# Row maxima by a transposing transfer of three BF16 parts, exponentials four slots behind, FFN weights summed one part per slot

## The chip, the cores and the metric

The kernel runs on one core of a Trainium2 chip. A core has five engines that follow their own instruction streams and wait for each other by semaphores: TensorE (PE, with its weight loads shown as PEld), VectorE (DVE), ScalarE (ACT), GpSimd (POOL) and SyncE (SP, which here only issues transfers). Transfers are carried out by 16 DMA engines. The metric is the device time of one execution in microseconds (us); lower is better. A run's time is a little longer than the span of the instructions that the profiler records.

## The reference, cut to what matters

One transformer layer in FP32 on x of 2 x 1024 tokens x 512: attention with 32 heads of 16, then an FFN with quantised activations and ternary weights.

```python
q, k, v = (proj(w_q), proj(w_k), proj(w_v))          # from layernorm(x), 32 heads of 16
scores = jnp.einsum('bhqd,bhkd->bhqk', q, k) / jnp.sqrt(jnp.float32(D_K))
attn = jax.nn.softmax(scores, axis=-1)
out = jnp.einsum('bhqk,bhkd->bhqd', attn, v)
x = x + jnp.einsum('bse,oe->bso', out.transpose(0, 2, 1, 3).reshape(B, S, HIDDEN), w_o)
xq = int4_quant(layernorm(x))                        # per token
w_q = jnp.clip(jnp.round(w / (mean(abs(w)) + EPS)), -1.0, 1.0)   # for each of the three FFN weights
gate = jnp.square(jax.nn.relu(bitlinear(xq, w_gate, s_gate)))
inter = int8_quant(bitlinear(xq, w_up, s_up) * gate)
x = x + bitlinear(inter, w_down, s_down)
```

What matters for this case: softmax subtracts, in exact arithmetic, any number per query; the kernel subtracts the row's maximum, which it must know before the first exponential of that row. The FFN weights need mean(abs(w)) over the whole matrix before they can be made ternary.

## The kernel before, in words

The attention is cut into 32 steps (batch, half of the queries, group of 8 heads, and one of two head sets of 4). A step has 512 queries, 1024 keys and 4 heads, one head per strip of 32 rows of the PE array. Each step is cut into 8 slots. The main loop runs over slots T, and in each slot it writes out, for every engine, the work of three steps at different stages:

- **Maxima** of step n in slots 8n to 8n+7 (`max_mm` L590, `max_reduce` L600): per slot two PSUM tiles `psm` of 128 queries x 2 heads x 512 keys. PE writes them with queries on the partitions (two passes, for a high and a low part of q), and DVE reduces each to negated maxima, collected in `pm`.
- **Maxima into rows** (`max_parts` L602-608, `max_rows` L610-617). The exponentials have keys on the partitions and queries along the free axis, so the maxima, which stand one query per partition, must be turned into rows. In slot 8n+8 DVE combines the two key halves into `m` and writes two FP32R parts (the rounded value and what is left) into columns 32r and 32r+1 of `mcols`. At the end of slot 8n+9 PE turns the four 128-column blocks by matmuls with an identity (`psn`, L613), in one of the three rotating PSUM tiles that `pse` and `psm` use, and ACT copies the result to `mrow` (L617).
- **Exponentials** of step n from slot 8n+LE, with LE = 8 + LEAD and LEAD = 2 (`exp_mm` L630, `exponentials` L634): two PSUM tiles `pse` per slot, each of 128 keys x 2 heads x 512 queries, in three passes l: k times the high and the low part of q, and as the last pass a row of ones times the two rows of `mrow`, which subtracts the maximum. ACT takes exp of a whole tile into `e`.
- **Values** one slot later (`weigh_values` L660): `pso` accumulates e times v, with a column of ones for the denominators. After the last slot of a step ACT copies it to `po`; `normalise` (L672-699) sends the denominators through memory and multiplies on POOL.

A slot is written in this order (main loop, L1400-1445): the loads that are due, `max_parts` where it is due, one mixed group of scores (`pse` of one half beside `psm` of the other, on disjoint row strips, passes interleaved), `pso` of the slot before, a short piece of other work, the second mixed group, `max_rows` where it is due, and then `fill.run`. In slots before LE there are only maxima, in the last LE slots only exponentials.

**Other work** is handed out by `Fillers`: projections (`psq`, `psk` L476, `psv` L533), the output projection (`psy` L847), the FFN (`pg`, `pu` L937, `py` L1006), each a generator that yields estimated PE time or a gap, counted in calls of `run`, of which a mixed slot makes two. `pace` spreads the PE time over the slots that are left, at least 960 and at most 1800 ns a slot. The due times contain LEAD.

**Loads.** `load_k` (L567) and `load_q` (L573) of step n are written at slot 8n-5 into `kst` (3 buffers) and `qst` (6, two per step), so they overwrite step n-3; all tiles wait by themselves for the last reader of the buffer. `load_v` (L578) is written at slot 8n+5 (8n+8 for n under 8). All of these, the transposing transfers `xqT` (L919) and `iqT` (L1000), the projections' weights (L457) and `normalise`'s transfers stand in one SP queue, in the order in which they are written; SP issues them one after the other, and a transfer that waits holds up those behind it. The DMA rings also take SP's transfers in order.

**FFN weights.** `weight_sums` (L757-776) loads 35 parts of 256 KB or less by POOL, ACT sums each one's absolute value, four loads ahead, with ("gap", 1) between parts; then follow `weight_means` and `weight_quant`.

`the_end` (L1043) is the last FFN, after all slots, by a planner of its own.

Of the kernel before, what the change touches and what calls it, by code (L numbers as in the profile page):

```python
# [10 lines left out]
F32 = mybir.dt.float32  # L11
F32R = mybir.dt.float32r
BF16 = mybir.dt.bfloat16
# [3 lines left out]
ALU = mybir.AluOpType  # L17
# [4 lines left out]
P = 128  # L22
# [211 lines left out]
def kernel(  # L234
# [28 lines left out]
    nc = tc.nc  # L263
# [6 lines left out]
    QB = 512  # L270
    NQ = S // QB
    TQ = QB // P
    FC = (I + P - 1) // P
    SCALE = 0.25
    LEAD = 2

    WARM = 24

    const = ctx.enter_context(tc.tile_pool(name="const", bufs=1))
    sb = ctx.enter_context(tc.tile_pool(name="sb", bufs=1))  # L280
    sp = ctx.enter_context(tc.tile_pool(name="sp", bufs=3))
# [13 lines left out]
    identr = const.tile([P, P], F32R, name="identr")  # L295
    nc.vector.tensor_copy(identr, eye)
    ident = identr.bitcast(F32)
    onesr = const.tile([P, P], F32R, name="onesr")
    nc.vector.memset(eye, 1.0)
    nc.vector.tensor_copy(onesr, eye)  # L300
# [10 lines left out]
    negmagic = const.tile([P, 1], F32, name="negmagic")  # L311
    nc.vector.memset(negmagic, -MAGIC)

    mcols = [const.tile([P, TQ, P], F32R, name=f"mcols{k}") for k in range(2)]
    vst = [const.tile([P, 2, 4, 4, 32], F32, name=f"vst{k}") for k in range(1)]
    for m in mcols:
        nc.gpsimd.memset(m.bitcast(F32), 0.0)
    for v in vst:
        for s in range(2):
            nc.gpsimd.memset(v[:, s, :, :, 16 * (1 - s) : 16 * (1 - s) + 16], 1.0)  # L320
# [15 lines left out]
    def scores_psum(name):  # L336
        return ps_s.tile([P, 2, QB], F32, tag="s", name=name)
# [222 lines left out]
    pm, mrow, probs = {}, {}, {}  # L560
# [41 lines left out]
    def max_parts(n):  # L602
        m = sp.tile([P, TQ, 4], F32, tag="m", name=f"m_{n}")
        p = pm.pop(n)
        nc.vector.tensor_tensor(m, p[:, :, 0, :], p[:, :, 1, :], ALU.min)
        cols = mcols[n % 2].rearrange("p t (r c) -> p t r c", r=4)
        nc.vector.tensor_copy(cols[:, :, :, 0], m)
        nc.vector.tensor_tensor(cols[:, :, :, 1], m, cols[:, :, :, 0].bitcast(F32), ALU.subtract)

    def max_rows(n):  # L610
        ps = scores_psum(f"psn_{n}")[:, 0, :]
        for t in range(TQ):
            nc.tensor.matmul(  # L613
                ps[:, t * P : (t + 1) * P], mcols[n % 2][:, t, :], identr, start=True, stop=True
            )
        mrow[n] = sb.tile([P, QB], F32R, tag="mrow", name=f"mrow_{n}", bufs=2)
        nc.scalar.copy(mrow[n], ps)  # L617

    probs = {}

    def exp_mm(n, i, j, ps, l):
        for r in (2 * j, 2 * j + 1):
            rows = slice(32 * r, 32 * r + 32)
            if l < 2:
                left, right = kst[n][rows, i * P : (i + 1) * P], qst[n][l][rows, :]
            else:

                rows = slice(32 * r, 32 * r + 2)
                left, right = onesr[rows, :], mrow[n][rows, :]
            nc.tensor.matmul(ps[:, r % 2, :], left, right, start=(l == 0), stop=(l == 2))  # L630

    def exponentials(n, i, j, ps):
# [117 lines left out]
    def load_raw(m, i, name):  # L750
        ap, parts = mats[m]
        c, n, rows, cols = parts[i]
        t = sb.tile([P, 512], F32, tag="raw", name=f"{name}{m}_{c}_{n}", bufs=4)
        nc.gpsimd.dma_start(t[:rows, :cols], ap[c * P : c * P + rows, n : n + cols])
        return t

    def weight_sums():  # L757
        for m in range(3):
            wsum[m] = const.tile([P, 12], F32, name=f"wsum{m}")
            nc.gpsimd.memset(wsum[m], 0.0)  # L760
        todo = [(m, i) for m in range(3) for i in range(len(mats[m][1]))]
        raw = deque()
        for k in range(len(todo) + 4):
            if k >= 4:
                m, i = todo[k - 4]
                c, n, rows, cols = mats[m][1][i]
                junk = sb.tile([P, 512], BF16, tag="junk", name=f"junk{m}_{i}", bufs=1)
                nc.scalar.activation(
                    junk[:rows, :cols],
                    raw.popleft()[:rows, :cols],  # L770
                    AF.Abs,
                    accum_out=wsum[m][:rows, i : i + 1],
                )
            if k < len(todo):
                raw.append(load_raw(*todo[k], "raw"))
            yield ("gap", 1)

    def weight_means():
        tot = sp.tile([P, 3], F32, tag="wtot", name="wtot")
# [499 lines left out]
    for k, ap in enumerate((s_gate, s_up, s_down)):  # L1279
        t = const.tile([P, 1], F32, name=f"scale{k}")  # L1280
# [5 lines left out]
    ps = scores_psum("warm")  # L1286
    for k in range(WARM):
        nc.tensor.matmul(
            ps[:, k % 2, :], onesr, mcols[0].rearrange("p t c -> p (t c)"), start=True, stop=True
        )  # L1290
    fill.kind = "s"
    now(firsts[0])
# [40 lines left out]
    for b in range(B):  # L1333
# [12 lines left out]
        for g in range(NG):  # L1346
            n = first_step[b, 0, g]
# [8 lines left out]

    LE = NT + LEAD
    NSTEP = len(steps)
# [8 lines left out]
    for b in range(B):  # L1367
        for h in range(NQ):
            last = b == B - 1 and h == NQ - 1

            by = min(NT * (first_step[b, h, 0] + 4 * NG) + 40, NT * NSTEP + LEAD)
            ready = [f"norm_{b}_{h}_{g}" for g in range(NG - last)] + ["wo"]
# [3 lines left out]
            for tiles in ((0, 1), (2, 3)) if b == B - 1 else (tuple(range(TQ)),):  # L1376
                name = f"out_{b}_{h}_{tiles[0]}"
# [21 lines left out]
    left = 0.0  # L1399
    for T in range(LE + NT * NSTEP + 1):  # L1400
        fill.slot = T
        ne, ie = divmod(T - LE, NT)
        nm, im = divmod(T, NT)
        nw, iw = divmod(T - LE - 1, NT)

        fill.scores = int(T < LE - 1 or T >= NT * NSTEP)

        n = T // NT + 1
        if 1 < n < NSTEP and T == load_slot(n):
            b, h, g, s = steps[n]  # L1410
            fill.ensure(f"k_{b}_{g}_0", f"k_{b}_{g}_1", f"q_{b}_{g}_{h}")
            places(n)
            load_k(n)
            load_q(n)
        n = (T - 5) // NT
        if 0 <= n < NSTEP and T == due_v(n):
            b, h, g, s = steps[n]
            fill.ensure(f"v_{b}_{g}_0", f"v_{b}_{g}_1")
            load_v(n)
        if im == 0 and 0 < nm <= NSTEP:  # L1420
            max_parts(nm - 1)
        exps = [(ne, ie, j) for j in range(2)] if 0 <= ne < NSTEP else []
        maxs = [(nm, im, j) for j in (1, 0)] if nm < NSTEP else []
        mixed = bool(exps and maxs)
        if mixed:
            scores(exps[:1], maxs[:1])
        elif exps:
            scores(exps, [])
        if 0 <= nw < NSTEP:
            weigh_values(nw, iw)  # L1430
            if iw == NT - 1 and nw % 2 and nw < NSTEP - 1:
                b, h, g, _ = steps[nw]
                fill.add(f"norm_{b}_{h}_{g}", normalise(nw), (), "back")
            if iw == NT - 1 and nw == NSTEP - 2:
                fill.add("tokens", first_tokens(nw), (), "ffn", 0)
        feed()
        fill.run(100.0, short=True)
        if mixed:
            scores(exps[1:], maxs[1:])
        elif maxs:  # L1440
            scores([], maxs)
        if im == 1 and 0 < nm <= NSTEP:
            max_rows(nm - 1)
        share = min(max(fill.pace([w[4:] for w in ffns]), SHARE), MORE)
        left = fill.run(share + min(left, SHARE))

# [51 lines left out]
```

## Time and profile before

| | |
|---|---|
| median of 3 runs | 1182.28 us (1181.44 to 1182.52) |
| the profiled execution | 1181.5 us, span 1179.7 us, mean granted TensorE clock 0.999 |
| PE busy | 1154.8 us (98%) |
| DVE busy | 868.8 us (74%) |
| ACT busy | 686.8 us (58%) |
| POOL busy | 264.1 us (22%) |
| SP's transfers | 105.75 MB, 34.6% of the 16 DMA engines' span |
| `psn` matmuls, L613 | 128, busy 21.2 us, mean 288 ns |
| `mrow` copies on ACT, L617 | 32, busy 18.6 us, mean 582 ns |
| `pse<-mrow` matmuls, L630 | 1024, busy 203.9 us, mean 396 ns |

How to read it: busy time of PE is the union of modelled intervals; matmuls overlap, so a mean of 396 ns is a latency and not a price. The price of a matmul is read from the step from one start to the next. "Idle before" tells how long an engine stood before an instruction and what ended that; it costs nothing on an engine that is not the bottleneck.

### The profile page before, as it was taken

The page shows a single profiled execution, that of the slowest core. Times are in us where ns is not written, and L with a number is a line of the kernel's source. Part 1 is how long each engine was busy: PE and PEld are TensorE (multiplying, and loading weights), DVE is VectorE, ACT ScalarE, POOL GpSimd, SP SyncE. Part 2 cuts the span into 40 slices and gives each one's busy share as a digit, 9 for nine tenths or more (in the row PEclk, how much of TensorE's full clock was granted, in tenths as well). Part 3 has the DMA queues.
Part 4 walks back from the last instruction along what each step waited for, and adds up shares of the span by engine and source line. Part 5 has one row for each costly group of instructions (what it writes and reads, how often), then busy time and mean ns, then how long its engine had stood idle before and what let it go on. Part 6 is the DMA issues. An engine that isn't in the chain of part 4 may idle for free.

```text
span 1179.7 us, 21990 instructions
## 1 busy us (share of the span) xinstructions
PE 1154.8 (98%) x8922; PEld 522.5 (44%) x8922; DVE 868.8 (74%) x1261; ACT 686.8 (58%) x878; POOL 264.1 (22%) x319
## 2 busy tenths in 40 slices
PE   8899999999999999999999999999999999999998
PEld 5454444544444444544444445444444433444344
DVE  6765577898876677788866665786988788888467
ACT  2058765556565556566665555465666555665746
POOL 3224336465501101221011011022110001220111
PEclk9999999999999999999999999999999999999999
DMA  5666765556623323443633324244442516362300
GB/s 157 174 183 194 249 197 176 172 190 197 194 93 96 103 55 110 113 95 77 94 86 121 124 59 147 84 130 138 84 97 60 89 53 83 58 81 55 79 9 37
DMA packets 97099, 135.35 MB, mean 115 GB/s; under 512 B 34829, under 2 KB 54285, under 8 KB 96997
## 3 DMA queue, kind: packets, MB, share of 16 engines
q1 hardware_dynamic: 87204, 105.75, 34.6%
q0 software_dynamic: 9792, 28.19, 7.7%
q8 instruction: 70, 1.15, 0.4%
q14 instruction: 33, 0.26, 0.1%
HBM read 89.25 MB, written 37.19 MB: 107 GB/s over the span
## 4 chain that ended last, share of the span: by engine, by line
PE 81%; DVE 5%; DMA 5%; issue 2%; POOL 2%; SPq 2%; ACT 2%; POOLq 0%; DVEq 0%; ACTq 0%
PE pse L630 25%; PE pso L660 18%; PE psm L590 9%; PE psv L533 4%; PE psk L476 4%; PE psy L847 4%; PE psq L476 4%; PE pu L937 2%; PE py L1006 2%; DVE pm L600 2%; PE pg L937 2%; DMA rden<-rD 1%; PE psn L613 1%; SPq L505 1%; PE end L1161 1%
## 5 line engine op out<-in xcount | busy, mean ns | idle before, releaser
L600 DVE TENSOR_REDUCE pm<-psm 128x2 f32<-128x1024 f32 x512 | 623.8, 1222 | 242.9 <-PE pse L630 146.0
L634 ACT ACTIVATE e<-pse 128x1024 f32<-128x1024 f32 x512 | 522.7, 1023 | 408.2 <-PE pse L630 307.3
L590 PE MATMUL psm<-kst,qst 32*128 32x512 f32 x2048 | 369.5, 444 | 7.3 <-DMA kst<-kD 3.8
L630 PE MATMUL pse<-qst,kst 32*128 32x512 f32 x2048 | 367.6, 442 | 3.9 <-DVE pm L600 3.1
L630 PEld LDWEIGHTS pse<-qst,kst 32*128 32x128 f32 x2048 | 149.2, 183 | 332.8 <-issue 199.7
L660 PE MATMUL pso<-e,v 128*32 128x512 f32 x2048 | 272.9, 605 | 0.0
L630 PE MATMUL pse<-mrow,onesr 2*128 2x512 f32 x1024 | 203.9, 396 | 0.0
L590 PEld LDWEIGHTS psm<-kst,qst 32*128 32x128 f32 x2048 | 151.3, 183 | 25.5 <-ACT e L634 10.8
L630 PEld LDWEIGHTS pse<-mrow,onesr 2*128 2x128 f32 x1024 | 94.5, 183 | 3.3
L951 POOL TENSOR_TENSOR g<-g 128x460 f32<-128x460 f32 (+1 forms) x36 | 34.7, 964 | 244.7 <-ACT g L947 237.4
L660 PEld LDWEIGHTS pso<-e,v 128*32 128x32 f32 x2048 | 40.4, 108 | 94.4 <-issue 93.7
L807 POOL TENSOR_SCALAR low<-raws,whalf 128x512 bf16<-128x512 f32 (+2 forms) x35 | 52.0, 1488 | 30.5 <-DMA raws<-in_wuT 8.1
L476 PE MATMUL psq<-xnT,wq 128*128 128x512 f32 x112 | 57.8, 626 | 0.0
L533 PE MATMUL psv<-wv,xnT 128*128 128x128 f32 x384 | 53.2, 285 | 0.0
L533 PEld LDWEIGHTS psv<-wv,xnT 128*128 128x128 f32 x384 | 45.9, 191 | 12.5 <-issue 11.7
L847 PE MATMUL psy<-wo,OT 128*128 128x512 f32 x96 | 49.6, 625 | 0.0
L476 PE MATMUL psk<-xnT,wk 128*128 128x512 f32 x96 | 49.5, 624 | 0.0
L699 POOL TENSOR_TENSOR OT<-po,rden 128x512 f32<-128x512 f32 x15 | 19.2, 1278 | 99.5 <-PE pse L630 52.8
L547 POOL DMA_DIRECT2D vD<-vst x30 | 16.7, 559 | 110.5 <-ACT vst L545 107.8
L909 POOL TENSOR_SCALAR xn<-x,mv,a 128x512 f32<-128x512 f32 x12 | 25.1, 2089 | 71.5 <-DVE a L885 71.5
L937 PEld LDWEIGHTS <-xqT 128*128 128x128 bf16 x288 | 22.4, 98 | 37.8 <-issue 23.8
L937 PE MATMUL pg<-wg,xqT 128*128 128x460 fp8e4 (+1 forms) x144 | 34.2, 360 | 0.0
(227 smaller groups left out, 945.1 us busy)
## 6 DMA issues: line engine op xcount, KB each, us to landing
v<-vD SPq DMA_DIRECT2D x32, 512.0 KB
kst<-kD SPq DMA_DIRECT2D x31, 512.0 KB
qst<-qD SPq DMA_DIRECT2D x60, 256.0 KB
vD<-vst POOLq DMA_DIRECT2D x30, 256.0 KB, 5.7
qD<-hi_q SPq DMA_DIRECT2D x28, 256.0 KB
qD<-lo_q SPq DMA_DIRECT2D x28, 256.0 KB
x<-in_x SPq DMA_DIRECT2D x20, 256.0 KB
rden<-rD SPq DMA_DIRECT2D x15, 256.0 KB
```

What stands on the lines that cost most here:

```text
L476: nc.tensor.matmul(ps, w[:, c, :], xnT[b, h][:, c, :], start=(c == 0), stop=(c == KC - 1))
L533: nc.tensor.matmul(ps[:, i * P : (i + 1) * P], xnT[b, half][:, c, i * P : (i + 1) * P], w[:, c, :], start=(c == 0), stop=(c == KC - 1),)
L590: nc.tensor.matmul(ps[:, r % 2, :], qst[n][l][rows, t * P : (t + 1) * P], kst[n][rows, kh * QB : (kh + 1) * QB], start=(l == 0), stop=(l = ...
L600: nc.vector.tensor_reduce(pm[n][:, t, kh, 2 * j : 2 * j + 2], ps, AX.X, ALU.max, negate=True)
L630: nc.tensor.matmul(ps[:, r % 2, :], left, right, start=(l == 0), stop=(l == 2))
L634: nc.scalar.activation(e, ps, AF.Exp, scale=SCALE)
L660: nc.tensor.matmul(acc[n][32 * r : 32 * r + 32, :], vt[n][:, i, r, :], e[r // 2][:, r % 2, :], start=(i == 0), stop=(i == NT - 1),)
L807: nc.gpsimd.tensor_scalar(low, w, h[:rows, m, 1:2], None, ALU.is_lt)
L847: nc.tensor.matmul(ps, OT[b, h, g][:, i * P : (i + 1) * P], wo[g], start=(g == 0), stop=(g == NG - 1),)
L909: nc.gpsimd.tensor_scalar(xn, xt, mean, a, ALU.subtract, ALU.mult)
L937: nc.tensor.matmul(ps, xT[:, c, :], w[:, c, n : n + size], start=(c == 0), stop=(c == KC - 1))
L951: nc.gpsimd.tensor_tensor(g2[j], g2[j], g2[j], ALU.mult)
```

## The change

LEAD goes from 2 to 4, so every exponential stands four slots behind the last maxima of its step instead of two, and the due times that contain LEAD move with it. The maxima are written as three BF16 parts instead of two FP32R ones: `max_parts` now has five instructions (combine, BF16 copy, rest, BF16 copy of the rest, second rest) where it had three, and ends with a transposing transfer of `mcols` (128 x 512 BF16) to `mrow` on SP. `max_rows`, with its four matmuls, its PSUM tile and ACT's copy, is gone. The last pass of the exponentials has BF16 operands: three rows of `mrow` and three rows of BF16 ones. `weight_sums` has ("gap", 2) between parts, which in mixed slots is one part per slot instead of two. The warm-up matmuls use the BF16 tiles.

```diff
-    LEAD = 2
+    LEAD = 4
@@
+    onesb = const.tile([P, P], BF16, name="onesb")
+    nc.vector.memset(onesb, 1.0)
@@
-    mcols = [const.tile([P, TQ, P], F32R, name=f"mcols{k}") for k in range(2)]
+    mcols = [const.tile([P, TQ * P], BF16, name=f"mcols{k}") for k in range(2)]
@@ def max_parts(n):
-        cols = mcols[n % 2].rearrange("p t (r c) -> p t r c", r=4)
+        cols = mcols[n % 2].rearrange("p (t r c) -> p t r c", t=TQ, r=4)
+        rest = sp.tile([P, TQ, 4], F32, tag="rest", name=f"rest_{n}", bufs=1)
         nc.vector.tensor_copy(cols[:, :, :, 0], m)
-        nc.vector.tensor_tensor(cols[:, :, :, 1], m, cols[:, :, :, 0].bitcast(F32), ALU.subtract)
-
-    def max_rows(n):
-        ps = scores_psum(f"psn_{n}")[:, 0, :]
-        for t in range(TQ):
-            nc.tensor.matmul(
-                ps[:, t * P : (t + 1) * P], mcols[n % 2][:, t, :], identr, start=True, stop=True
-            )
-        mrow[n] = sb.tile([P, QB], F32R, tag="mrow", name=f"mrow_{n}", bufs=2)
-        nc.scalar.copy(mrow[n], ps)
+        nc.vector.tensor_tensor(rest, m, cols[:, :, :, 0], ALU.subtract)
+        nc.vector.tensor_copy(cols[:, :, :, 1], rest)
+        nc.vector.tensor_tensor(cols[:, :, :, 2], rest, cols[:, :, :, 1], ALU.subtract)
+        mrow[n] = sb.tile([P, TQ, P], BF16, tag="mrow", name=f"mrow_{n}", bufs=2)
+        nc.sync.dma_start_transpose(mrow[n], mcols[n % 2])
@@ def exp_mm(n, i, j, ps, l):
-                rows = slice(32 * r, 32 * r + 2)
-                left, right = onesr[rows, :], mrow[n][rows, :]
+                rows = slice(32 * r, 32 * r + 3)
+                left, right = onesb[rows, :], mrow[n][rows].rearrange("p t q -> p (t q)")
@@ def weight_sums():
-            yield ("gap", 1)
+            yield ("gap", 2)
@@ the warm-up
-            ps[:, k % 2, :], onesr, mcols[0].rearrange("p t c -> p (t c)"), start=True, stop=True
+            ps[:, k % 2, :], onesb, mcols[0], start=True, stop=True
@@ the main loop
-        if im == 1 and 0 < nm <= NSTEP:
-            max_rows(nm - 1)
```

## The prediction

> **What bounds the kernel now.** First the page's busy times, then the waits of PE, then the chain of work that ended last, then PE's timeline over three neighbouring slots, then SP's timeline.
>
> ```profile
> PE 1154.8 (98%) x8922; PEld 522.5 (44%) x8922; DVE 868.8 (74%) x1261; ACT 686.8 (58%) x878; POOL 264.1 (22%) x319
> ...
> PE 81%; DVE 5%; DMA 5%; issue 2%; POOL 2%; SPq 2%; ACT 2%; POOLq 0%; DVEq 0%; ACTq 0%
> ```
> ```profile
> PE psm L590 <- DMA kst<-kD: 3.8, 1, 3.8
> PE warm L1288 <- DVE lowrow L304: 3.6, 1, 3.6
> PE psm L590 <- ACT e L634: 3.2, 5, 0.9
> ```
>
> PE waits for others some 20 us in all, and the longest of it is one late `kst`. So the kernel is a row of PE instructions, and a slot costs what PE does in it. The timeline of slots 96 to 98 shows this to a hundredth (starts in us; each slot opens with a `pse<-qst,kst`):
>
> ```profile
> 423.57 0.50 PE L630 MATMUL pse<-qst,kst 32*128 32x512 f32 x2
> ...
> 428.28 0.50 PE L630 MATMUL pse<-qst,kst 32*128 32x512 f32 x2
> ...
> 430.17 0.50 PE L630 MATMUL pse<-qst,kst 32*128 32x512 f32 x2
> ...
> 431.09 0.66 PE L613 MATMUL psn<-identr,mcols 128*128 128x128 f32 x4
> 431.59 1.07 PE L847 MATMUL psy<-wo,OT 128*128 128x512 f32 x2
> 432.60 0.50 PE L630 MATMUL pse<-qst,kst 32*128 32x512 f32 x2
> ...
> 434.50 0.50 PE L630 MATMUL pse<-qst,kst 32*128 32x512 f32 x2
> 434.74 0.50 PE L590 MATMUL psm<-kst,qst 32*128 32x512 f32 x2
> 434.83 0.41 PE L630 MATMUL pse<-qst,kst 32*128 32x512 f32 x2
> 435.06 0.40 PE L630 MATMUL pse<-mrow,onesr 2*128 2x512 f32 x1
> ...
> 435.40 1.13 PE L847 MATMUL psy<-wo,OT 128*128 128x512 f32 x2
> 436.46 0.49 PE L630 MATMUL pse<-qst,kst 32*128 32x512 f32 x2
> ```
>
> Slot 96 (two `psy` matmuls) takes 4.71 us, slot 97 (`psn` and one `psy`) 4.32, slot 98 (one `psy`) 3.86. A mixed group (434.50 to 435.40) takes 0.90 us: three passes of `pse` in a chain, steps of 0.33 and 0.23, then 0.34 to the next shape. All 246 mixed slots fall on such prices: without other work 2.95, and 0.86 for each further matmul of 512 FP32 columns.
>
> **Part 1: `psn` goes.** Slot 97 against 98 prices it at 0.46; over the run, like slots with and without it differ by 0.45 (4.30 against 3.86, 4.34 against 3.90). Thirty lie in mixed slots, 13.5 us; one among maxima alone and one among exponentials alone, 0.35 each. **-14.2 us**. The 21.2 us of L613's busy time is not the price, because its latency overlaps the next matmuls. ACT loses 32 copies of 582 ns, 18.6 us, off the path: ACT is 58% busy.
>
> **Part 2: two more DVE instructions a step.** Three become five; the new ones are like L607 (207 ns) and L608 (230 ns), so 32 x 0.44 = 14 us on DVE. They stand ahead of slot 8n+8's reductions. DVE's reduction (1222 ns, two a slot, 2.44 of some 3.9 us) idles 243 us before it; the reductions cover the cost only while this lasts. Between 0 and +14; taken 0, since those waits are PE's.
>
> **Part 3: the way to `mrow`.** After the last reduction (1.2 us) five small DVE instructions (1.0), the transfer's issue on SP (the like-sized `xqT`, L919, 1.21 at the median, 7.55 once), landing 4.5 us after the issue at the median by the trace's semaphore events, 14.2 at worst. That is some 8 us, and four slots give 15.5. Taken 0; a transfer as slow as the worst would hold the third pass some 2 us, and with it PE. The wait has another side: SP now stands at each slot 8n+8 until DVE is done. Before, SP ran ahead: step 1's `v` was issued at 73.5 us, 13.7 us before its slot began. What stands behind it are weights (L457) used at least two slots later, and stores; priced in part 5. The 32 issues are 39 us of SP's time, which mostly waits.
>
> **Part 4: LEAD 4.** Mixed slots fall from 246 to 244; maxima alone and exponentials alone gain two slots each. The two mixed slots (10 and 11) cost 3.85 and 3.88. As slots of maxima alone they are DVE's: two reductions and a little, 2.6 (36 to 40 us: 2.66 to 2.79 with twice the other work), 5.2. Two slots of exponentials alone with nothing beside cost 1.90 and 2.15 near 1105 us; taken 3.8. 5.2 + 3.8 - 7.7 = **+1.3**. No reason excludes a gain: with other work in them these late slots cost 1.65 plus that work, so between +0.8 and +1.8.
>
> **Part 5: the loads of `kst` and `qst`.** With LEAD 4 the last exponentials of step n-3 stand in slot 8n-5, the same slot at whose head step n's load is written, where before they stood in 8n-7. So the load can start two slots later than before. SP's timeline for step 14, whose load waited for exactly that event before:
>
> ```profile
> 464.05 0.57 SPq L567 DMA_DIRECT2D kst<-kD  x1
> 464.66 1.11 SPq L573 DMA_DIRECT2D qst<-qD  x2
> 465.87 3.57 SPq L680 DMA_DIRECT2D dD<-po  x2
> ```
>
> The last `qst` lands at 478.9, 14.8 us after 464.05 (last semaphore event of that transfer). Step 14's maxima begin at 490.3, and the exponentials of slot 107 (8n-5) end at 472.6: from there, where the load now starts, 17.6 us remain. For steps 10 to 31 the loads take 13.9 to 19.9, median 14.8, and the window measured in this way is 16.4 to 21.6, median 17.6: mostly hidden with 2 to 3 us to spare. For steps 3 to 9 the loads take 17.0 to 24.8, because FFN weights travel beside them or their `qD` stores land late, and windows are 16.7 to 18.9. I take 3 us of stall at step 4 (its `q` store lands at 139.5, with 1 MB of x ahead in the rings), 1 each at 6 and 8, and 4 at step 9: the changed program's order puts batch 1's first `wv` behind step 9's loads and uses it in slot 70, some 12.5 us after those can start, while a transfer behind them lands when they do, 16 to 17 later. **+9**, between 0 (every load as in steps 10 to 31) and +35 (rival A). What is late next, behind the load in SP's queue, are `dD`, `rD` and `rden`; `normalise` moves by the same two slots.
>
> **Part 6: weight sums at half the rate.** ACT takes 626 + 193 ns for a part, two a slot beside two exponentials of 1023 ns: 3.7 of 3.9 us, and it waits for the raw loads too. Slots 20, 27 and 29 are 0.5, 0.8 and 0.9 longer than like slots. **-2**, between 0 and -2.5. The means come 19 slots later (slot 51, not 32, in the program's order), yet the first `pg` stands in slot 115 against 114: the FFN waits for attention, not for its weights.
>
> **Part 7: the BF16 pass.** 1024 matmuls keep 512 columns. The row for FP32R is the step 434.83 to 435.06, 0.23; `py` (BF16 weights, FP8 moving) steps by 0.216. So the pass saves 0.014 at most in 488 mixed groups, -7; and as the maxima's chain ends within 0.02 of it in half the groups, 0 is nearest. From above: a change of shape costs 0.107 beyond streaming (0.323 to 0.216); if a change of type beside FP32R on the other strips cost that once a group, +52. At 1138.47 an FP32 matmul is followed by BF16 ones after 0.429, the same as by FP32, so I take 0.
>
> ```profile
> L630 PEld LDWEIGHTS pse<-mrow,onesr 2*128 2x128 f32 x1024 | 94.5, 183 | 3.3
> ...
> L937 PEld LDWEIGHTS <-xqT 128*128 128x128 bf16 x288 | 22.4, 98 | 37.8 <-issue 23.8
> ```
>
> These weight loads begin when the second pass begins, 0.23 before their matmul, so 183 ns are hidden and 98 gain nothing. The Trainium skill, "TensorE: Matmul & The Clock Gate", section "Weight-path perf modes", says that weights of 128 columns and not FP32 load about twice as fast; if loads were on the path this would be 1024 x 85 ns, 87 us less, and the sum 1089. The skill's "TensorEngine Tiling (Array Packing)", section "Key Properties", speaks of a drain when the tiling mode changes; the strips stay 32 rows here, and no row of this trace mixes types on strips.
>
> **The sum.** -14.2 + 1.3 + 9 - 2 = -5.9 against the profiled execution's 1181.5 (span 1179.7 and 1.8 around it): 1175.6. The median of the runs stands 0.8 above that execution; I say 1176.
>
> **Rivals.**
> A, slower: the loads end last. If their rings also carry what part 5 shifts beside them (`v`, stores), each of 29 steps is bound by load and not by window. It decides from 17.6 us a load; break-even with the gains is 0.5 us a step beyond it, 18.1. At 18.8 each loses 1.2: +35 for the +9, 1202. For it: 17.0 to 24.8 in steps 3 to 9. Against: 14.8 after them.
> B: BF16 beside FP32R drains the array once a group, +52: 1228. For it: nothing in the trace mixes them. Against: 1138.47.
> C: the pass steps by 0.216 and no load is late: -7 and -9, 1160.
> D: `mrow` lands late, the new wait in place of the old one; at 2 us in a third of the steps +21, 1197. Against it 8 us of 15.5. The gain of `psn` itself can't fail to appear: its instructions are gone.
>
> **How the numbers follow.** Forecast 0.60 (own range 1166 with no stalls to 1184 with 18), A 0.15, B 0.08, C 0.12, D 0.05. A measurement of this kernel tells 0.2%, 2.4 us, from no change. Of the forecast 0.54 lies below 1180 and 0.06 within; with C faster 0.66; A and D give 0.01 to "same" and 0.19 to slower, B 0.08. The range reaches from C to A, 1160 to 1202.
>
> **What would show it.** Right: slots 8n+9 cost 3.86 like their neighbours, mixed groups still 0.90, PE's waits list `kst`, `qst` or `wv` for some 10 us. Wrong: PE waits for `mrow`; groups above 0.95; `psm<-` DMA waits of an us or more at most steps.

## The result, and the profile after

The changed kernel takes **1210.86 us** (median of four runs, 1205.29 to 1214.48) against 1181.86 for the kernel before in the same comparison: a ratio of **1.0245, 95% interval 1.0202 to 1.0287**, slower by 29 us. Forecast was 1176, with a range of 1160 to 1202. The profiled execution took 1211.93 us, with a span of 1210.2.

The page of the changed kernel, where it answers to the lines shown of before (busy times; the row of the granted TensorE clock in 40 slices; the chain that ended last):

```profile
PE 1171.4 (97%) x8794; PEld 520.2 (43%) x8794; DVE 877.8 (73%) x1326; ACT 671.5 (55%) x846; POOL 265.2 (22%) x319
...
PEclk9899999897958999999999999999999999999999
...
PE 81%; DMA 10%; DVE 3%; ACT 2%; SPq 1%; issue 1%; POOL 1%; POOLq 0%; ACTq 0%; DVEq 0%
```

PE has 128 matmuls fewer and is busy 16.6 us *longer*. The reason stands in the second line: from the 8th to the 13th slice the granted clock dips, down to 5 tenths. Transfers hold 10% of the chain that ended last, where it was 5%.

First, did the change do what it says? PE's timeline over slot 113, a slot 8n+9, where `psn` stood before:

```profile
528.63 0.49 PE L628 MATMUL pse<-qst,kst 32*128 32x512 f32 x2
528.80 0.49 PE L592 MATMUL psm<-kst,qst 32*128 32x512 f32 x2
528.97 0.40 PE L628 MATMUL pse<-qst,kst 32*128 32x512 f32 x2
529.14 0.39 PE L592 MATMUL psm<-kst,qst 32*128 32x512 f32 x2
529.20 0.39 PE L628 MATMUL pse<-mrow,onesb 3*128 3x512 bf16 x2
529.52 1.06 PE L658 MATMUL pso<-e,v 128*32 128x512 f32 x8
...
532.49 0.50 PE L628 MATMUL pse<-qst,kst 32*128 32x512 f32 x2
```

The slot takes 3.86 us (528.63 to 532.49), like its neighbours; before, slot 113 took 4.31. The mixed group takes 0.89 and the BF16 pass steps by 0.23 (528.97 to 529.20), as FP32R did. The gain is there.

Now PE's waits, the longest first:

```profile
PE psv L535 <- DMA wv<-in_wvT: 6.2, 1, 6.2
PE pse L628 <- DVE pm L602: 5.9, 4, 3.0
PE psm L592 <- ACT e L632: 5.6, 7, 0.9
PE psm L592 <- DMA qst<-qD: 4.3, 3, 2.0
PE psm L592 <- DMA kst<-kD: 3.2, 1, 3.2
```

(The 3.2 us at `kst` is step 1's, 3.8 before; the waits for ACT, 0.9 at most, were 3.2 in sum before.) New are `qst` of steps 4 and 6, 2.05 us each; `wv` in slot 70, 6.2; and 3.0 and 1.9 for DVE, at 272.5 and 434.7 us, where no wait for DVE's `pm` was over 1.3 before. Between 70 and 1100 us PE stands still for 22.0 us, against 8.5 before: 13.5 us more, not half of what the result asks for. The rest shows in the clock by stage. The rows are stretches of the span, with their length, busy time of PE, PEld, DVE, ACT and POOL with their instructions, the granted clock, and transfers:

```profile
160.00:220.00 60.00, 59.79 (x498) 29.15 (x494) 39.12 (x42) 42.92 (x70) 15.92 (x24) 1.00 0.58 169
220.00:232.00 12.00, 10.16 (x42) 3.12 (x42) 4.01 (x7) 3.06 (x5) 0.69 (x2) 0.57 0.48 139
...
272.00:287.00 15.00, 14.48 (x62) 4.61 (x62) 7.41 (x9) 3.68 (x4) 9.83 (x9) 0.54 0.62 185
...
333.00:375.00 42.00, 39.68 (x208) 17.83 (x208) 21.35 (x34) 13.57 (x16) 12.62 (x13) 0.51 0.34 109
375.00:436.00 61.00, 58.74 (x463) 26.72 (x460) 47.82 (x55) 32.77 (x37) 32.31 (x32) 1.00 0.51 137
...
440.00:1200.00 760.00, 753.30 (x5869) 327.69 (x5868) 577.37 (x905) 453.47 (x545) 110.42 (x113) 1.00 0.38 91
```

Each of these stretches at about half clock goes with one of the waits, which end at 221.8, 272.5 and 335.3. In 333 to 375 PE is busy 39.7 of 42 us and does 208 matmuls, 5.0 per us, against 7.6 in 375 to 436. One can see it begin:

```profile
328.73 0.39 PE L592 MATMUL psm<-kst,qst 32*128 32x512 f32 x2
335.32 2.08 PE L535 MATMUL psv<-wv,xnT 128*128 128x128 f32 x8 [6.20 <-DMA wv<-in_wvT]
337.32 0.79 PE L628 MATMUL pse<-qst,kst 32*128 32x512 f32 x2
...
344.40 0.79 PE L628 MATMUL pse<-qst,kst 32*128 32x512 f32 x2
```

Slot 71 opens at 337.32 and slot 72 at 344.40: 7.07 us for a slot that costs 3.89 elsewhere (slot 106, the same work). The `pse` matmul shows 0.79 where it was 0.50.

The trace's record of the granted clock gives the stretches exactly. They come in pieces of 3.41 us. Five waits, five stretches at 0.5: 2.05 us, then 3.4; 2.05, then 10.2; 2.99, then 13.7; 6.20, then 41.0; 1.93, then 3.4. Together 71.7 us, in 68.8 of which PE was busy; half of that, **34.4 us**, is work lost. So the profiled execution comes out:

| | before | after |
|---|---|---|
| profiled execution | 1181.5 | 1211.9 |
| PE idle, 70 to 1100 us | 8.5 | 22.0 |
| work lost at clock 0.5 (half the busy time there, after 60 us) | 0 | 34.4 |
| the rest | 1173.0 | 1155.5 |

The rest is 17.5 us shorter. The change gained about what it should, and lost 48 us to waits and to the slow clock after them.

Why are these transfers late? SP's timeline at step 9's load, with the `wv` of slot 70 behind it:

```profile
316.46 0.57 SPq L569 DMA_DIRECT2D kst<-kD  x1
317.08 1.11 SPq L575 DMA_DIRECT2D qst<-qD  x2
318.23 5.24 SPq L459 DMA_DIRECT2D wv<-in_wvT  x1
323.57 3.22 SPq L689 DMA_DIRECT2D rD<-den  x1
```

The load starts where the last exponentials of step 6 end (slot 67). Its last `qst` lands at 334.0, 17.5 us later, `wv` behind it at 335.3, and PE has waited since 329.1. The two waits for DVE are another path. The chain that leads to PE at 272.52, in order of time (start, length, what):

```profile
251.28 11.54 DMA rD<-den
...
262.84 3.88 DMA rden<-rD
...
266.80 0.28 POOL OT L697
...
268.64 1.58 POOL low L805
...
271.26 1.22 DVE pm L602
...
272.52 0.79 PE pse L628 x2
```

`normalise` sends the denominators out and in again; the store takes 11.5 us to land. POOL's multiplication for `OT` (L697) waits for that, POOL's `low` (L805), a piece of the weights' quantisation, stands behind it, DVE's half of the quantisation (L807) waits for `low`, the reductions stand behind that on DVE, and PE has no free score tile. Each piece of work stands in front of the next in the order of its engine, and so a late transfer for an output that nobody needs soon stops PE.

### The profile page after: what moved, and what is told of

The parts are those of the page before. It is cut to its first block, busy times and chain, and to the rows that moved or that the text cites. A ratio compares the mean times of both kernels' runs of the same rounds, so it can differ in the third digit from the quotient of the medians.

```text
span 1210.2 us, 21810 instructions
## 1 busy us (share of the span) xinstructions
PE 1171.4 (97%) x8794; PEld 520.2 (43%) x8794; DVE 877.8 (73%) x1326; ACT 671.5 (55%) x846; POOL 265.2 (22%) x319
## 4 chain that ended last, share of the span: by engine, by line
PE 81%; DMA 10%; DVE 3%; ACT 2%; SPq 1%; issue 1%; POOL 1%; POOLq 0%; ACTq 0%; DVEq 0%
PE pse L628 26%; PE pso L658 19%; PE psm L592 9%; PE psq L478 4%; PE psy L845 4%; PE psv L535 4%; PE psk L478 3%; PE pu L935 3%; PE pg L935 3%; PE py L1004 2%; DMA qst<-qD 2%; DMA rD<-den 2%; DMA qD<-lo_q 2%; DMA wv<-in_wvT 1%; DVE pm L602 1%
## 5 line engine op out<-in xcount | busy, mean ns | idle before, releaser
L592 PE MATMUL psm<-kst,qst 32*128 32x512 f32 x2048 | 378.7, 455 | 13.7 <-ACT e L632 5.6
L628 PE MATMUL pse<-qst,kst 32*128 32x512 f32 x2048 | 374.7, 451 | 6.2 <-DVE pm L602 5.9
L628 PEld LDWEIGHTS pse<-qst,kst 32*128 32x128 f32 x2048 | 152.9, 187 | 344.0 <-issue 205.8
L658 PE MATMUL pso<-e,v 128*32 128x512 f32 x2048 | 280.6, 621 | 0.0
L628 PE MATMUL pse<-mrow,onesb 3*128 3x512 bf16 x1024 | 200.8, 395 | 0.0
L949 POOL TENSOR_TENSOR g<-g 128x460 f32<-128x460 f32 (+1 forms) x36 | 34.4, 956 | 227.6 <-ACT g L945 227.6
L628 PEld LDWEIGHTS <-onesb 3*128 3x128 bf16 x1024 | 49.9, 94 | 56.8 <-issue 36.5
L535 PE MATMUL psv<-wv,xnT 128*128 128x128 f32 x384 | 57.1, 298 | 6.2 <-DMA wv<-in_wvT 6.2
L478 PE MATMUL psq<-xnT,wq 128*128 128x512 f32 x112 | 62.2, 669 | 0.0
L805 POOL TENSOR_SCALAR low<-raws,whalf 128x512 bf16<-128x512 f32 (+2 forms) x35 | 52.7, 1506 | 21.6 <-DVE wu L807 8.3
L535 PEld LDWEIGHTS psv<-wv,xnT 128*128 128x128 f32 x384 | 49.1, 202 | 16.4 <-issue 9.6
L697 POOL TENSOR_TENSOR OT<-po,rden 128x512 f32<-128x512 f32 x15 | 19.1, 1272 | 126.2 <-DMA rden<-rD 62.0
L492 POOL CAST hi_q<-full_q 128x512 fp32r<-128x512 f32 x14 | 8.5, 608 | 128.0 <-ACT full_q L491 128.0
L549 POOL DMA_DIRECT2D vD<-vst x30 | 16.6, 556 | 80.5 <-ACT vst L547 77.3
```

Of the source, the lines that this page charges most:

```text
L478: nc.tensor.matmul(ps, w[:, c, :], xnT[b, h][:, c, :], start=(c == 0), stop=(c == KC - 1))
L535: nc.tensor.matmul(ps[:, i * P : (i + 1) * P], xnT[b, half][:, c, i * P : (i + 1) * P], w[:, c, :], start=(c == 0), stop=(c == KC - 1),)
L592: nc.tensor.matmul(ps[:, r % 2, :], qst[n][l][rows, t * P : (t + 1) * P], kst[n][rows, kh * QB : (kh + 1) * QB], start=(l == 0), stop=(l = ...
L658: nc.tensor.matmul(acc[n][32 * r : 32 * r + 32, :], vt[n][:, i, r, :], e[r // 2][:, r % 2, :], start=(i == 0), stop=(i == NT - 1),)
L805: nc.gpsimd.tensor_scalar(low, w, h[:rows, m, 1:2], None, ALU.is_lt)
L949: nc.gpsimd.tensor_tensor(g2[j], g2[j], g2[j], ALU.mult)
```

## The experiments

Three explanations were held against each other: **theory 1**, the longer lead makes the loads late; **theory 2**, SP is held at each transposing transfer, and what stands behind it travels beside the next loads; **theory 3**, the slower weight sums put weights, quantisation and `wo` there. And for the second half of the loss: does a wait of PE really cost more than its length? Ratios are to the kernel before in the same comparison, with 95% intervals.

### The longer lead alone (b_lead4)

```diff
-    LEAD = 2
+    LEAD = 4
```

in the kernel before.

> The kernel before with LEAD = 4 and nothing else (psn, FP32R parts and the weight sums as before). Theory 1 (late loads, then a halved clock): with LEAD 4 the loads of kst and qst wait for exponentials in the same slot 8n-5, PE waits at a few places for 2 to 6 us, and after each such wait the granted clock is 0.5 for one or more stretches of 3.4 us. The changed kernel lost 55.7 us in its mixed slots in this way over its own slot prices, so this kernel is slow too: 1205 to 1240, with a granted clock below 0.99. Theory 2 (the transposing transfers in SP's queue hold the loads up): without them nothing is late, 1183 (+1.3 for the longer lead) and clock 0.999. Theory 3 (weight sums at half rate put their loads beside the attention's loads): 1183 as well, since the sums keep their rate here.

Measured: 1196.42 us, ratio 1.0146 (1.0131 to 1.0161), clock 0.993. PE's waits:

```profile
PE pse L630 <- DVE pm L600: 4.9, 6, 2.3
PE psm L590 <- DMA qst<-qD: 4.1, 3, 2.6
```

The lead alone is slower, by 17 us, and waits for `qst` are there without any transposing transfer: its last `qst` lands 2.0, 3.1 and 1.1 us after the maxima of steps 3, 4 and 6 have begun. But 17 us is less than theory 1 had (1205 or more): with the gain of `psn`, 14 us, the changed kernel would stand at some 1182. Theory 1 holds for a part of the loss, and is not all.

### A lead of three (a_lead3)

```diff
-    LEAD = 4
+    LEAD = 3
```

in the changed kernel.

> The changed kernel with LEAD = 3: the last reader of step n-3's buffers stands in slot 8n-6, so the loads written at the head of slot 8n-5 need not wait, and start one slot, some 3.7 us, earlier. Theory 1: the loads that were late by 2.0, 2.0 and, with wv behind them, 6.2 us are in time or nearly; slot prices without stalls sum to about 1156, and with the 10 us that the kernel before also loses over them 1166: 1158 to 1175, clock 0.99 or more. The row mrow has three slots, 11.6 us, for a way of 8 us. Theory 2 and theory 3: transfers and weight sums are as in the changed kernel, so 1200 to 1212.

Measured: 1199.48, ratio 1.0191 (1.0154 to 1.0228); the interval overlaps that of the changed kernel. A miss for theory 1. The load of step 4 is issued after 130.5 us, only 1.3 earlier than in the changed kernel, since it is now held by what precedes it in SP's queue, takes 24.3 us instead of 20.7, and ends 3.0 us after the step's maxima have begun, as before (2.9); those of steps 6 and 8 end 2.3 and 2.4 after, and `wv` costs 4.7.

### Loads over all DMA engines (a_wide, then a_wide2)

```diff
@@ def step_k(n), load_q(n): 128 rows that lie together
-        return kD[b, g].rearrange("(r s e) q -> s r e q", r=4, s=2)[s]
+        return kD[b, g].rearrange("(s e) q -> s e q", s=2)[s]
...
-            rows = qD[b, g, h][l].rearrange("(r s e) q -> s r e q", r=4, s=2)[s]
+            rows = qD[b, g, h][l].rearrange("(s e) q -> s e q", s=2)[s]
@@ the first step's copies, v and wo in the new order of heads
-                            src = part[32 * r + 16 * s : 32 * r + 16 * s + 16, :].bitcast(F32)
+                            src = part[64 * s + 16 * r : 64 * s + 16 * r + 16, :].bitcast(F32)
...
-        src = ps.rearrange("p (t r s d) -> p t r s d", t=4, r=4, s=2)
+        src = ps.rearrange("p (t s r d) -> p t r s d", t=4, r=4, s=2)
...
-            nc.sync.dma_start(t, woT[g * P : (g + 1) * P, :])
+            rows = woT[g * P : (g + 1) * P, :].rearrange("(s r d) e -> r s d e", s=2, r=4)
+            for r in range(4):
+                nc.sync.dma_start(t[32 * r : 32 * r + 32, :], rows[r])
```

> The changed kernel with LEAD = 4, but step s of a group takes heads 4s to 4s+3 instead of every second head, so that each load of kst and qst reads 128 rows that lie together and can be spread over all 16 DMA engines, where each such load posts only 5 completion events (4 engines and the end) in the trace of the changed kernel. v, wo and the first step follow the new order of heads. Theory 1: the three loads of a step take 7 us or less instead of 14 to 20, none is late though LEAD is still 4: 1155 to 1170, clock 0.99 or more. Theory 2 (the transposing transfer holds SP) and theory 3 (raw loads): the wait of SP or the rate of the sums has not changed, so most of the loss stays: 1190 to 1212.

Measured: 1175.40, ratio 0.9950 (0.9927 to 0.9972), just above what theory 1 had and far below the others. No wait for `kst`, `qst` or `wv` is left after the start, with LEAD still 4; but the sixteen small `wo` transfers, a side effect of this edit, made `rD` late, and PE waited 10.1 us for DVE by the chain shown above. The next run takes `wo` through memory instead:

```diff
@@ def load_wo(), instead of the four small transfers for each group
+        woD = [dram.tile([P, H], F32, name=f"woD{g}") for g in range(NG)]
+        for g in range(NG):
+            rows = woT[g * P : (g + 1) * P, :].rearrange("(s r d) e -> r s (d e)", s=2, r=4)
+            nc.gpsimd.dma_start(woD[g].rearrange("(r s d) e -> r s (d e)", s=2, r=4), rows)
+            yield ("gap", 2)
+        yield ("gap", 6)
...
+            nc.sync.dma_start(t, woD[g])
```

> As the run with loads of 128 rows that lie together (LEAD 4), but wo's rows are brought into the new order by one transfer from memory to memory for each group, spread over 8 calls of run, and then loaded as before in four transfers; in the run before 16 small wo transfers held SP for 18 us, rD and rden came late, POOL stood 15.7 us, DVE behind POOL's low 11.4 us, and PE 10.1 us, with 13.7 us at a clock of 0.5 after it. If that wait was the side effect of the wo transfers, it goes, and with it 10.1 and about 5 us of slow clock: 1156 to 1162, clock 0.997 or more. If it is of the changed kernel's own (rden late in slot 58 there too, 3.0 us), a part of it stays: 1165 to 1175.

Measured: **1160.38** (1159.56 to 1161.04), ratio **0.9832** (0.9814 to 0.9849). From its page, the clock and the chain:

```profile
PEclk9999999999999999999999999999999999999999
...
PE 91%; DVE 4%; ACT 2%; DMA 1%; issue 1%; SPq 1%; DVEq 0%; ACTq 0%
```

Transfers have 1% of the chain and the clock never dips. A `kst` load lands 3.6 us after its issue at the median, with 16 completion events, where it took 10.1 with 5; the three loads of a step take 5.1 instead of 15.3 (median of steps 10 to 31), and in these steps are done 10 us or more before their use, in steps 3 to 9 at least 6.5. The lead, the transfer on SP and the slower sums are all still there. So what all three did, they did by way of transfers that were too slow for the new order.

The Trainium skill, "DMA: Bandwidth & Descriptors", section "Why a DMA increments its semaphore by 16 and not by 1", says that a transfer is spread over the largest number of engines up to 16 that divides the slowest dimension of its access patterns. The loads' slowest dimension was 4 and is 128 here, and the events, 5 against 16, agree with it.

### Undoing the other parts, one at a time (a_lead2, a_gap1, a_late)

```diff
@@ a_lead2
-    LEAD = 4
+    LEAD = 2
@@ a_gap1, in weight_sums
-            yield ("gap", 2)
+            yield ("gap", 1)
@@ a_late: the transfer where psn stood, at the end of slot 8n+9
-        nc.sync.dma_start_transpose(mrow[n], mcols[n % 2])
...
+        if im == 1 and 0 < nm <= NSTEP:
+            nc.sync.dma_start_transpose(mrow[nm - 1], mcols[(nm - 1) % 2])
```

> The changed kernel with LEAD = 2, so that only the BF16 rows by transfer and the slower weight sums remain. LEAD 4 alone cost the kernel before 17 us, and LEAD 3 left the changed kernel at 1199. Theory 1 (the lead alone makes loads late): loads start as in the kernel before, so nothing is late but mrow, whose way of some 8 us is as long as the two slots: 1165 to 1185. Theory 2 (SP, held at each transposing transfer until DVE has finished the step, lets what stands behind it travel beside the next loads): 1190 to 1205, and PE's waits name qst again at steps 4, 6 and 8. Theory 3 (sums at half rate): the same 1190 to 1205.

> The changed kernel with the weight sums at their old rate (gap 1), LEAD 4 and the transfer as they are. Theory 3 (the slower sums, with quantisation and wo later, cause what LEAD 4 does not explain): 1180 to 1190. Theories 1 and 2: 1203 to 1212, within what separates two executions.

> The changed kernel with the transposing transfer written at the end of slot 8n+9, where psn stood, instead of at the head of slot 8n+8. SP then reaches it when DVE has long finished, and what was written in slots 8n+8 and 8n+9 is issued ahead of it. mrow still has two slots and a half, some 10 us, for an issue and landing of some 6. Theory 2: SP is no longer held, and what remains is the 17 us that LEAD 4 cost the kernel before, less the 14 of psn: 1182 to 1192. Theories 1 and 3: 1203 to 1212.

Measured: LEAD 2 1192.24 (1185.52 to 1201.05), ratio 1.0108 (1.0056 to 1.0160). Old rate of the sums 1193.25 (1184.88 to 1201.79), 1.0112 (1.0055 to 1.0169). Late transfer 1198.35, 1.0160 (1.0125 to 1.0196). Against the changed kernel's 1.0245 each takes back 10 to 16 us, none 29. LEAD 2 falls where theories 2 and 3 had it, the two others between the ranges of all three: none of the parts is the cause by itself. The profiled execution was the slowest of four with LEAD 2 and with the old rate, 9 us above the median, so the waits below are those of an execution above the usual. What is left of each without waits and slow clock is the changed kernel's, 1155.0, 1155.2 and 1158.1 against 1155.5; the waits change places. LEAD 2 waits 2.1 us for `qst` of step 4, 5.1 for `wv`, and 2.2 and 6.7 for DVE; the old rate waits 9.1 for `qst` in five places; the late transfer keeps the 7.2 for `wv`. PE names no wait for `mrow` even with LEAD 2.

### The slower sums alone (b_gap2)

```diff
-            yield ("gap", 1)
+            yield ("gap", 2)
```

in `weight_sums` of the kernel before.

> The kernel before with the weight sums at one part per slot (gap 2) and nothing else. Undoing this part alone took 18 us off the changed kernel. If the sums' later end is a cause of its own (35 raw loads, the quantisation and wo beside the loads of steps 4 to 8), this kernel is slow too: 1190 to 1200. If it only costs where loads have no margin left (steps 4 and 6 had 0.1 and 0.5 us before, the others 5 to 12): 1180 to 1188, with a wait for qst at step 4 or 6.

Measured: 1191.13, ratio 1.0094 (1.0076 to 1.0111). Theory 3's number, but only partly its place: no wait for `qst`. PE waits 2.0 us for `wv` in slot 70 and 2.1 and 4.4 for DVE, by the chain of `rden`. POOL's timeline shows the longer one:

```profile
383.99 1.57 POOL L807 TENSOR_SCALAR low<-raws,whalf 128x512 bf16<-128x512 f32 x1
396.72 1.27 POOL L699 TENSOR_TENSOR OT<-po,rden 128x512 f32<-128x512 f32 x1 [11.16 <-DMA rden<-rD]
397.94 0.59 POOL L754 DMA_DIRECT2D raws<-in_wdT  x1
398.57 1.57 POOL L807 TENSOR_SCALAR low<-raws,whalf 128x512 bf16<-128x512 f32 x1
```

POOL stood 11.2 us for `rden`, with `low` behind it. In the kernel before POOL also stood up to 12.4 us for `rden`, but DVE never waited over 0.8 us for `low`.

### The kernel before on fast loads (b_wide2)

The two edits above, in the kernel before.

> The kernel before (LEAD 2, psn, sums at the old rate) with the loads of 128 rows that lie together and wo reordered in memory, as the run of the changed kernel that took 1160.4. If late loads are what LEAD 4, the transfer and the slower sums brought, then the kernel before has little to gain: its profile names 3.8 us at one kst and no other load: 1173 to 1182, and the change, both on fast loads, is worth 13 to 20 us. If the loads on four engines cost something in every kernel, by contention rather than by lateness, this one falls as far as the changed one did, to 1165 or below.

Measured: 1175.58, ratio 0.9958 (0.9943 to 0.9973). It gains 5 us, mostly the wait for step 1's `kst`. **On loads that are in time the change is worth 1175.6 - 1160.4 = 15.2 us** (14.9 by the two ratios).

### What a wait of PE costs (b_stall, b_stall2, b_stall3)

```diff
@@ the main loop of the kernel before, after the second mixed group
+        if T + 3 in STALLS:
+            st = sb.tile([P, 512], F32, tag="raw", name=f"stall_{T}", bufs=4)
+            nc.gpsimd.memset(st, 0.0)
+        if T in STALLS:
+            two = scores_psum(f"stall_{T}")[:, 0, :]
+            nc.tensor.matmul(two[:, :P], ident, st[:, :P], start=True, stop=True)
+            for cols in STALLS[T]:
+                nc.gpsimd.tensor_scalar(st[:, :cols], st[:, :cols], 0.5, None, ALU.mult)
+            nc.tensor.matmul(two[:, :P], ident, st[:, :P], start=True, stop=True)
```

`STALLS` names the slots, and for each the POOL instructions that PE waits for; the second and third run take another buffer for `st`.

> The disputed cost by itself: the kernel before, with eleven waits of chosen length put into PE's queue, at the end of slots 134, 146, ... 254. Each is a matmul, then one to four POOL instructions on the tile that it read (128 to 2048 columns, by the 1.57 us of L805 about 0.4, 0.8, 1.6, 2.4, 3.1, 4.7, 0.8, 1.6, 3.1, 6.3, 0.4 us), then a matmul that reads the tile again. Theory 1: a wait of about 2 us or more is followed by stretches of 3.4 us at a granted clock of 0.5, in which PE's work takes twice as long, so that such a wait costs 1.7 us or more on top of itself; waits of 1 us or less cost only themselves. In sum 25 us of waits and 5 us of matmuls, and at least 10 us on top: above 1222. The rival, that a wait costs its own length (the clock record being a by-effect): about 1212, and the slots after each wait keep their 3.9 us.

> As the run with eleven waits put into PE's queue, but six equal waits of some 3.2 us at the end of slots 50, 60, ... 100, where the work beside attention is projections in FP32; the waits of 2.6, 3.2, 4.2, 4.8 and 6.4 us in the later slots, beside the FFN, were each followed by 6.8 us at a clock of 0.5, while the changed kernel stayed at 0.5 for 13.7 and 41.0 us after waits of 3.0 and 6.2 us in slots 58 and 70. If the length is set by the wait alone: 6.8 us (3.4 to 10.2) after each, and some 1181 + 6 x (3.3 + 0.5 + 3.4) = 1224. If the work beside decides: 13.7 us or more after some or most, 1240 or above.

> As the runs with waits put into PE's queue, at the places and of the lengths that the changed kernel had: 3.2 us at the end of slot 58, 6.3 us at the ends of slots 70, 82, 94 and 106. Seventeen put-in waits so far were followed by at most 10.2 us at a clock of 0.5; the changed kernel stayed there for 13.7 us after slot 58 and for 41.0 after slot 70. If a longer wait, or the work of these slots, draws the stretch out: 20 us or more after at least two of the four long waits, 1181 + 29 + 40 = 1250 or above. If not, 6.8 to 10.2 after each: 1181 + 29 + 5 x 3.5 = 1228, and the length of the 41.0 us stretch stays unexplained by the wait before it.

Measured, by one execution each: 1232.8, 1221.8 and 1224.0. PE stands 28.9, 18.6 and 28.7 us longer than before, and loses 16.8, 17.1 and 12.4 us of work to the slow clock on top; the remaining 1 to 6 us hold the matmuls of the waits. (Five of the six waits of the second run took 3.2 us, one 4.9.) One wait of the second kernel, by stretches: the wait, what follows it, and after that.

```profile
381.67:384.89 3.22, 0.01 (x1) 0.00 (x0) 1.24 (x2) 0.70 (x1) 2.98 (x2) 0.95 0.00 0
384.89:391.40 6.51, 6.51 (x36) 3.79 (x38) 1.58 (x2) 1.02 (x1) 0.00 (x0) 0.50 0.00 0
391.40:396.00 4.60, 4.60 (x50) 2.82 (x42) 2.71 (x3) 2.95 (x4) 0.00 (x0) 1.00 0.14 14
```

After 3.2 us without work PE runs 6.5 us at clock 0.50, 36 matmuls against 50 in the shorter stretch that follows. No load is late there and no transfer moves, so the wait alone does it. Of the 19 put-in waits of 1.6 us and more, 18 were followed by 3.4 (twice), 6.8 (13 times) or 10.2 us (three times) at 0.5; one of 1.65 us and two of 1.0 by none. The rival, that a wait costs its own length, is out. But the length of the wait hardly sets the stretch: 2.6 us and 6.4 us both brought 6.8. And the last run, with waits in the changed kernel's slots and at least as long as its own (3.3 us in slot 58, 7.8 in slot 70), brought 6.8 after slot 58 and 10.2 after slot 70, where the changed kernel had 13.7 and 41.0.

Whether a stretch begins at all depends on where the wait falls. The clock changes only at the ends of the record's pieces of 3.41 us, and the wait of 1.65 us lies across two of them, in each of which PE worked more than 2.4 us:

```profile
970.19:973.60 3.41, 2.72 (x26) 1.01 (x20) 2.27 (x2) 2.57 (x3) 0.59 (x1) 1.00 0.27 90
973.60:977.01 3.41, 2.45 (x20) 1.26 (x24) 0.29 (x2) 0.09 (x1) 1.43 (x3) 1.00 0.44 146
```

In all sixteen traces cut in this way, from 60 to 1095 us and at full clock, 44 pieces had PE busy for 54% or less, and half clock followed every one. Of those with 56 to 75%, 7 were followed and 55 were not; one more stretch came after a piece with 88%. (Before 60 us, near step 1's `kst`, five pieces with 42 to 53% were not followed.) So waits of one length can cost different times: in the first run 1.64 us brought 3.4 us at half clock and 1.65 us none.

The Trainium skill, "TensorE: Matmul & The Clock Gate", section "Part 1: The HAM clock gate", says that the clock is halved after an idle window of about 3.4 us and returns after a busy one. The pieces of 3.41 us agree. But waits of 1.6 to 2.1 us were enough here, and the return took two pieces as a rule and up to twelve; the measurement decides.

### The best of it (a_wide2l3), and the sums' rate where no load is late (a_wide2l3g1)

LEAD = 3 in the changed kernel on fast loads; then also ("gap", 1).

> The changed kernel on fast loads (1160.4) with LEAD = 3. If loads no longer set anything, only the ends change: one slot of maxima alone and one of exponentials alone less, 0.65 by the earlier working, and mrow has three slots for a way of 8 us: 1158 to 1161. If mrow is late in some steps, PE waits for it: 1165 or more.

> The changed kernel on fast loads with LEAD = 3 (1159.2), and the weight sums at their old rate. If the sums' rate only mattered because it put weights, quantisation and wo beside late loads, it is worth nothing here: 1157 to 1162. If summing two parts a slot on ACT holds PE (slots 20, 27 and 29 of the kernel before were 0.5 to 0.9 longer than like slots): 1161 to 1164. If earlier weights let the FFN start earlier and fill more slots: below 1157.

Measured: **1159.24** (1159.00 to 1159.74), ratio **0.9821** (0.9807 to 0.9836), the fastest of all, 21 us below the kernel before; and 1164.63, 0.9870 (0.9852 to 0.9888) with the old rate. The slower sums are worth 5.4 us on fast loads with LEAD 3, though they cost the kernel before 11. At the old rate PE waits 2.0 us for ACT at 130.8 us, and a stretch of 3.4 us at clock 0.5 follows.

The profiled executions, but for those with put-in waits, by the same account (idle between 70 and 1100 us; lost is half of PE's busy time at clock 0.5 after 60 us):

| kernel | execution | idle | lost | rest |
|---|---|---|---|---|
| before | 1181.5 | 8.5 | 0 | 1173.0 |
| before, LEAD 4 | 1196.6 | 16.4 | 6.8 | 1173.4 |
| before, slower sums | 1193.9 | 16.7 | 7.7 | 1169.5 |
| before, fast loads | 1175.6 | 8.2 | 0 | 1167.4 |
| after | 1211.9 | 22.0 | 34.4 | 1155.5 |
| after, LEAD 3 | 1197.5 | 22.6 | 20.3 | 1154.6 |
| after, LEAD 2 | 1201.1 | 24.0 | 22.1 | 1155.0 |
| after, old rate of the sums | 1201.8 | 23.4 | 23.2 | 1155.2 |
| after, late transfer | 1199.6 | 24.0 | 17.5 | 1158.1 |
| after, wide loads, `wo` in small transfers | 1172.3 | 17.9 | 2.4 | 1152.0 |
| after, fast loads (`wo` through memory) | 1160.9 | 8.3 | 0 | 1152.6 |
| the same, LEAD 3 | 1159.2 | 7.8 | 0 | 1151.4 |
| the same, LEAD 3, old rate of the sums | 1165.2 | 10.4 | 1.7 | 1153.1 |

Among the five forms of the changed kernel on the old loads the idle time is nearly the same, 22 to 24 us; what differs is how long the clock stayed low, 17.5 to 34.4 us of lost work.

## Why the prediction was wrong, step by step

**Part 1, `psn` goes: right.** Slots 105, 113 and 121 took 4.35, 4.31 and 4.29 us and take 3.89, 3.86 and 3.68. With parts 4 and 6 the forecast was -14.2 + 1.3 - 2 = -14.9; where loads are in time, the change measures -15.2. That these agree so closely is partly luck: on fast loads with LEAD 3 the sums alone give -5.4 where part 6 had -2, and what takes back those 3 us no run shows.

**Parts 2, 3 and 7: right.** No wait for `mrow` at any lead, groups still 0.89, so rivals B and D did not happen, although 1210.9 lies nearest to B's and A's numbers. Nor did C, although the kernel on fast loads comes to C's 1160: the pass still steps by 0.23 us, and fast loads give the kernel before 5 us too. (The FP32 matmul that part 7 places at 1138.47 starts at 1138.90; the 0.43 us from it to the BF16 one is right.) A transposing transfer lands 2.5 us after its issue at the median, 9.3 at worst, quicker than the 4.5 and 14.2 that part 3 took from `xqT`. Part 3 named the wait on the other side, SP held until DVE is done, and gave it no price: writing the transfer later takes back some 10 us, so it had one.

**Part 4: right in sign.** LEAD 3 against 4 on fast loads is 1.1 us apart, where half of 1.3 was forecast; the intervals overlap.

**Part 6: wrong in the sign that counted.** -2 was forecast for ACT's relief. That relief exists and is larger (-5.4 on fast loads), but alone on the kernel before the slower sums cost 11 us: the quantisation moves into slots where POOL waits for `rden`, and DVE and PE behind it. Part 6 asked only when the FFN needs its weights, not what the moved work would stand behind.

**Part 5 is the step that failed: +9 for the loads.** The places were nearly right: `qst` of step 4 (2.05 for the 3 forecast), of step 6 (2.05 for 1), step 8 (nothing for 1), `wv` in slot 70 (6.2 for 4). The waits that came by way of `rD`, 3.0 and 1.9, were not priced: part 5 only named `rD` and `rden` as late next. All in all PE stands 13.5 us longer; +9 was that, a little small. **What was left out is the clock**: 34.4 us of work lost after these waits. The trace of before held the row for it: after its 3.8 us wait for `kst`, which ends at 55.7 us, the granted clock is 0.5 for 3.4 us (12 matmuls, then 26 in the same time), and the mean of 0.999 hid it.

```profile
57.20:60.60 3.40, 3.40 (x12) 0.85 (x10) 1.62 (x2) 0.00 (x0) 0.00 (x0) 0.51 0.11 31
60.60:64.00 3.40, 3.40 (x26) 1.83 (x22) 2.66 (x3) 1.19 (x3) 0.04 (x1) 0.99 0.22 73
```

One such row does not show how long the clock can stay low, but it shows that a wait is not priced by its length.

Rival A had the right suspect and the wrong form: loads that end last in each of 29 steps. In steps 10 to 31 the changed kernel's loads land 2.5 us early at the median; the late ones of steps 4 and 6, and the `wv` behind step 9's, sufficed, together with the waits by way of `rD`.

What stays open: why the clock stayed at 0.5 for 41.0 us once, and for 13.7 to 24 us in other forms, with PE busy all the while, when put-in waits of like length at like places brought 10.2 at most.

## What to carry to other kernels

On a kernel that PE bounds, price each new wait of PE by its length plus what the clock takes after it, here 2 to 3 us of lost work for a wait put in, and 20 for one in the changed kernel; read the granted clock by stage and not its mean. Before moving work later in a tuned order, look for the transfers with no margin (here 0.1 and 0.5 us in steps 4 and 6), and count their completion events: a load on 4 of 16 engines was a new order of the heads away from landing in little over a third of the time. When undoing any one of several small moves takes back only a part of the loss, ask what they share; here undoing them one by one only moved the waits.

## What the runs showed of the hardware

- Waits of PE of 1.6 us and more were followed by 3.4 us or a multiple of it at half clock, but for three (1.65 and 2.19 us in the first run with put-in waits, 2.79 us at step 1's `kst` in the changed kernel with the old rate of the sums). Put-in waits of 1.0 us were followed by none, but one wait of 1.39 us for ACT (lead of four alone) by 3.4 us.
- The clock changes on a grid of 3.41 us. From 60 to 1095 us each of the 44 pieces at full clock with PE busy for 54% or less was followed by half clock; with 56 to 75%, 7 of 62.
- The stretch does not grow with the wait: 6.8 us after 2.6 us and after 6.4 us, but 41.0 us once in the changed kernel.
- A `kst` load of 512 KB landed 10.1 us after its issue on 4 engines and 3.6 us on 16.
- A transposing transfer of 128 x 512 BF16 within SBUF took 1.23 us to issue and landed after 2.5 us at the median.
